# A two-level Strassen projection: another order of its products, two of its results combined in turn, and two reciprocals moved behind the score evictions

## The chip, the cores and the metric

The kernel runs on one core of a Trainium2 chip. The metric is the device time of one execution in microseconds. Below, PE is TensorE's matmul pipe and PEld its weight load, DVE is VectorE, ACT is ScalarE, POOL is GpSimd and SP is SyncE.

## The reference, cut to what matters

`x` has 64 graphs of 256 nodes with 512 features, `adj` is one 256 x 256 matrix shared by all. Everything is float32. Two layers with a residual each:

```python
h = relu(layernorm(x))
x = x + einsum('nm,bmd->bnd', adj, h) @ W0 + b0          # layer 0

h = relu(layernorm(x))                                    # layer 1, 8 heads of 64
q, k, v = h @ Wq + bq, h @ Wk + bk, h @ Wv + bv
scores = einsum('bqhd,bkhd->bhqk', q, k) / 8 + (1 - adj) * -1e9
x = x + einsum('bhqk,bkhd->bqhd', softmax(scores), v) @ Wo + bo
```

## The kernel before, in words

**Groups and halves.** The 64 graphs are worked on two at a time, in 32 groups (`NG`). Layer 0 runs over all groups first, and leaves its residual and its normalized, turned result in DRAM. Layer 1 then runs over the groups; it takes a little over 2000 us of the span, about 66.5 us for each group. This text is about layer 1.

**The projections.** Each 512 x 512 weight times the group's 512 x 512 activations is done with Winograd's form of Strassen's algorithm: seven products of half-size blocks in place of eight. `weight_sums` makes the weight sums s1 to s4, `Halves.sums` the activation differences t1 to t4. `project` (L447) does one level: P1 = a11 b11 goes to bank pa, and is read from there (u1) before more is added to it; a12 b21 makes result (0,0) with u1; s2 t2 is added to pa (u2 is read); s1 t1 goes to bank pc (c22 is read); s3 t3 is added to pa once more (u3 is read, and with c22 it makes result (1,1)); a22 t4 makes (1,0) with u3; s4 b22, added to pc, makes (0,1) with u2. In the kernel's listing P5 is the product s1 t1. A result's first index is the half of the output features, the second the graph of the pair. Because s2 t2 is added in the bank that u1 was read from, TensorE can start that product only when the reader of P1 is through.

For Q, K and V the reader is ScalarE (L756 with the bias, L777 a copy), which writes u into one of three buffers of the pool `tmp`. For the output projection (`post`, L791) the reader is VectorE, which adds the product to the residual in place (L600).

**The second level.** From group 4 on (`FIRST2`), the three products of Q, K and V that are used once (a12 b21, a22 t4, s4 b22) are themselves done by seven quarter-size products, in `project2` (L559), `product2` (L527, matmuls at L538) and `finish2` (L540). `product2` writes what several quarters share to a bank `shared`, the rest to the bank `own`. `finish2` then makes the result by five adds on VectorE (`add`, L599), each of which reads what the one before wrote: own plus u over 512 elements, a shared part onto 512, onto 384, onto 256, and the last onto 128 (or 256 for s4 b22, whose bank pc already held s1 t1).

**Attention.** A group has two halves of four heads, `qd` 0 and 1. `attend` (L849) sums the exponents over the keys on TensorE (pden, L856), multiplies them with V (pav, L863, into two banks `po`), reads the sums with ScalarE (L870) and makes reciprocals of them on VectorE, in four calls of 128 columns (L873). A closure `divide` is queued for the next tick: it multiplies `po` with the reciprocals (L880), gives its two banks back, has ScalarE add up the reciprocals for a check of range (L882), and starts the differences that the output projection needs. `score` (L814) makes the scores in banks (L824), moves each 128 x 512 bank to SBUF with scale and mask on VectorE (L829, eight evictions), subtracts a bound on GpSimd (L835), takes the exponent on ScalarE (L840) and adds pairs of keys on GpSimd (L847).

**Order.** All instructions are put in order by hand: each engine runs its own in the order in which the program makes them. Generators yield between products; `run` calls `tick` at each yield, and `after(n, f)` has f emitted n ticks later. For group g the main loop (L946) does: `attend(g, 0)`, `score(g, 1)`, a tick (so `divide` comes right behind the score), Q and K of group g+1, `attend(g, 1)`, `score(g+1, 0)`, a tick, V of group g+1, and the output projection `post(g)`. Around the end of that loop, group 31 has no next Q, K, V; `post(30)` runs in their place.

**Banks.** PSUM's eight banks are handed out first in, first out by `bank` and `give` while the program is made; an instruction that writes a bank waits on the chip for the last reader of its earlier tile.

The functions that the change touches, with what calls them:

Of the kernel before, what the change touches and what calls it, by code (L numbers as in the profile page):

```python
# [198 lines left out]
def kernel(  # L199
# [24 lines left out]
    NG = B // GB  # L224
# [21 lines left out]
    def bank(shape, name):  # L246
        i = free_banks.pop(0)
        t = psum.tile(shape, F32, tag=f"bank{i}", name=name)
        bank_of[id(t)] = (i, t)
        return t  # L250

    def give(t):
        free_banks.append(bank_of.pop(id(t))[0])
# [35 lines left out]
    def quarter(xt, i, k):  # L289

        return xt[:, k * NT:(k + 1) * NT, i * HF:(i + 1) * HF]
# [111 lines left out]
    W = {}  # L403
# [35 lines left out]
    def product(ps, s, a, halves, b, by_token, start=True, stop=True):  # L439
        for m in range(2):  # L440
            for c in range(2):
                w, y = s[a][:, c, :], halves.operand(b, c)
                lhs, rhs = (y[:, m * P:(m + 1) * P], w) if by_token else (w[:, m * P:(m + 1) * P], y)
                nc.tensor.matmul(ps[:, m, :], lhs, rhs, start=(start and m + c == 0), stop=(c == 1),  # L444
                                 skip_group_check=True)

    def project(s, halves, by_token, name, read, finish, first_half_first=False):  # L447


        def new(n):  # L450
            return bank([P, 2, N], f"{name}{n}")
        pa = new("a")
        product(pa, s, "a11", halves, "b11", by_token, stop=False)
        u1 = read(pa, 1)
        yield
        if first_half_first:
            pc = new("c")
            product(pc, s, "s1", halves, "t1", by_token, stop=False)
            c22 = read(pc, 0)
            yield  # L460
        pb = new("b")
        product(pb, s, "a12", halves, "b21", by_token)
        finish(pb, u1, 0, 0)
        give(pb)
        yield
        product(pa, s, "s2", halves, "t2", by_token, start=False, stop=False)
        u2 = read(pa, 2)
        yield
        if not first_half_first:
            pc = new("c")  # L470
            product(pc, s, "s1", halves, "t1", by_token, stop=False)
            c22 = read(pc, 0)
            yield
        product(pa, s, "s3", halves, "t3", by_token, start=False)
        u3 = read(pa, 3)
        finish(pa, c22, 1, 1)
        give(pa)
        yield
        pd = new("d")
        product(pd, s, "a22", halves, "t4", by_token)  # L480
        finish(pd, u3, 1, 0)
        give(pd)
        yield
        product(pc, s, "s4", halves, "b22", by_token, start=False)
        finish(pc, u2, 0, 1)
        give(pc)
        yield
# [6 lines left out]
    FIRST2 = 4  # L494
# [45 lines left out]
    def finish2(o, own, shared, u, by_token, fresh):  # L540

        def quarters(t):
            return t.rearrange("p m (n k) -> p (m n) k", k=P)

        def spread(i, n):
            return shared[:, i:i + 1, :].to_broadcast([P, n, P])
        add(o, own, u)
        q = quarters(o)
        lower = q[:, 1::2, :] if by_token else q[:, 2:4, :]
        right = q[:, 2:4, :] if by_token else q[:, 1::2, :]  # L550
        add(q, spread(0, 4), q)
        add(q[:, 1:4, :], spread(1, 3), q[:, 1:4, :])
        add(lower, spread(2, 2), lower)
        if fresh:
            add(right[:, 0, :], quarters(own)[:, 3, :], right[:, 0, :])
        else:
            add(right, spread(3, 2), right)

    def project2(n, halves, blocks, by_token, name, read, target):  # L559

        s = W[n]

        def new(i):
            return bank([P, 2, N], f"{name}{i}")

        def once(own, a, i, k, u, fresh):
            shared = bank([P, 4, P], f"{name}r")
            product2(own, shared, W2[n, a], blocks[ONCE[a]], by_token, fresh)
            finish2(target(i, k), own, shared, u, by_token, fresh)
            give(own)  # L570
            give(shared)

        pa = new("a")
        product(pa, s, "a11", halves, "b11", by_token, stop=False)
        u1 = read(pa, 1)
        yield
        pc = new("c")
        product(pc, s, "s1", halves, "t1", by_token, stop=False)
        c22 = read(pc, 0)
        yield  # L580
        product(pa, s, "s2", halves, "t2", by_token, start=False, stop=False)
        u2 = read(pa, 2)
        yield
        once(new("b"), "a12", 0, 0, u1, True)
        yield
        product(pa, s, "s3", halves, "t3", by_token, start=False)
        u3 = read(pa, 3)
        add(target(1, 1), pa, c22)
        give(pa)
        yield  # L590
        once(new("d"), "a22", 1, 0, u3, True)
        yield
        once(pc, "s4", 0, 1, u2, False)
        yield

    def partial(name, n):
# [2 lines left out]
    def add(o, ps, u):  # L599
        nc.vector.tensor_tensor(o, ps, u, op=ALU.add)  # L600
# [187 lines left out]
    def quarter_of(batch, i):  # L788
        return batch.rearrange("(t p) d -> p t d", p=P)[:, :, i * HF:(i + 1) * HF]

    def post(g):  # L791

        xt = X.pop(g)
        halves = HO.pop(g)
        done = []

        def read(ps, n):
            o = quarter(xt, *RESIDUAL[n])
            add(o, ps, o)

        def finish(ps, u, i, k):
            o = quarter(xt, i, k)
            add(o, ps, o)
            done.append(k)
            if g == NG - 1:
                nc.sync.dma_start(quarter_of(out[g * GB + k], i), o)
            elif done.count(k) == 2:
                nc.sync.dma_start(out[g * GB + k].rearrange("(t p) d -> p t d", p=P), xt[:, k * NT:(k + 1) * NT, :])

        yield from project(W["o"], halves, True, f"o_{g}", read, finish, first_half_first=g == NG - 1)  # L810

    A, AS = {}, {}

# [35 lines left out]
    def attend(g, qd):  # L849


        pd = bank([P, GN], f"pden_{g}_{qd}")
        po = [bank([P, GN], f"pav_{g}_{qd}_{f}") for f in range(2)]
        for b in range(GB):
            for h in range(4):
                nc.tensor.matmul(pd[h * 32:(h + 1) * 32, b * N:(b + 1) * N], ones[:, 0:32], AS[h // 2, b][:, h % 2, :],  # L856
                                 start=True, stop=True, tile_position=(0, h * 32))
        for b in range(GB):
            v = V[g][qd, b]
            for k in range(NT):  # L860
                for f in range(2):
                    for h in range(4):
                        nc.tensor.matmul(po[f][h * 32:(h + 1) * 32, b * N:(b + 1) * N],  # L863
                                         v[:, k, h * HD + f * 32:h * HD + f * 32 + 32],
                                         A[h // 2, b][:, (h % 2) * NT + k, :],
                                         start=(k == 0), stop=(k == NT - 1), tile_position=(0, h * 32))
        i = g * HQ + qd
        dens = act.tile([P, 2, GN], F32, tag="yT1", name=f"den_{g}_{qd}")
        den, rden = dens[:, 0, :], dens[:, 1, :]
        nc.scalar.activation(den, pd, AF.Identity, accum_out=stats[:, 0, i:i + 1])  # L870
        give(pd)
        for c in range(4):
            nc.vector.reciprocal(rden[:, c * P:(c + 1) * P], den[:, c * P:(c + 1) * P])  # L873
        if qd == 0:
            OT[g] = act.tile([P, DC, GN], F32, tag="r", name=f"oT_{g}")
            HO[g] = Halves(f"o_{g}", [OT[g][:, :, k * N:(k + 1) * N] for k in range(GB)], 1)

        def divide():
            for f in range(2):
                nc.vector.tensor_tensor(OT[g][:, 2 * qd + f, :], po[f], rden, op=ALU.mult)  # L880
                give(po[f])
            nc.scalar.activation(den, rden, AF.Identity, accum_out=stats[:, 1, i:i + 1])  # L882
            if g < NG - 2 or qd == 0:
                HO[g].sums(nc.gpsimd if g < NG - 1 else nc.vector, ("t1",) if qd == 0 else ("t2", "t3", "t4"))
            elif g == NG - 2:
                after(9, HO[g].sums, nc.gpsimd, ("t2", "t3", "t4"))
            else:
                HO[g].sums(nc.vector, ("t2",))
                after(1, HO[g].sums, nc.vector, ("t3", "t4"))

        after(1 if g < NG - 1 or qd else 8, divide)

    def run(gen, steps=99):
# [129 lines left out]
```

## Time and profile before

| what | value |
|---|---|
| time, median of 3 runs | 2771.95 us (2771.8 to 2772.26) |
| span of the profiled execution | 2769.3 us |
| L829 evictions, 512 of them | 310.2 us, 678 ns each |
| L873 reciprocals, 256 of 128 x 128 | 216.5 us, 908 ns each |
| L882 sums of the reciprocals, 64 | 40.3 us, 630 ns each |
| L870 sums over the keys, 64 | 38.2 us, 597 ns each |

A row of the timeline has the start, the length, the engine, the line, the operation, what it writes and reads, their shapes, and a count; rows of one kind that follow each other are merged, and lengths overlap a little where an engine starts the next instruction before the last has ended. What stands in brackets is idle time of the engine just before the row, and what ended it. Matmuls of float32 show as two rows each, so that 8 rows are a product's four matmuls of 256 columns. Lines named L600 are VectorE's add, whoever calls it: the names of the tiles tell the caller (q, k, v: `finish2`; x: the output projection).

### The profile page before, as it was taken

To read this page: it belongs to the slowest core of one execution; us is meant where nothing else is said; L and a number is where in the kernel's file an instruction comes from. 1 tells how busy PE (TensorE), PEld (TensorE's weight loads), DVE (VectorE), ACT (ScalarE), POOL (GpSimd) and SP (SyncE) were. 2 spreads that over 40 slices of the span, in tenths; PEclk is the share of its full clock that TensorE was granted. 3 is DMA by queue.
4 is the path that set the end of the run, shared out by engine and by line. 5 is a ranking of instruction groups with operands and counts; after the bars stand their busy time and mean duration, and the time that the engine had idled before them with its cause. 6 is when DMAs were issued, how large, how long until landed. Compare 5 with 4: busy or idle time off the path is not lost.

```text
span 2769.3 us, 47852 instructions
## 1 busy us (share of the span) xinstructions
PE 2690.7 (97%) x18684; PEld 2271.7 (82%) x18684; DVE 2002.4 (72%) x3789; ACT 875.6 (32%) x1537; POOL 1961.6 (71%) x1630
## 2 busy tenths in 40 slices
PE   8999999999999999999999999999999999999998
PEld 7888888887888888888888888888888888888886
DVE  7777777865446777777777777777777777777776
ACT  3434344343332222333222222222333222222221
POOL 6777776675777667777777777667777777666665
PEclk9999999999999999999999999999999999999999
DMA  7776666662111111111111112222211111111110
GB/s 187 191 192 166 160 169 161 172 151 68 46 47 46 47 47 47 47 47 47 47 47 46 47 47 54 57 60 56 51 47 47 47 47 47 47 47 47 47 47 32
DMA packets 281045, 210.78 MB, mean 76 GB/s; under 512 B 145904, under 2 KB 212976, under 8 KB 280816
## 3 DMA queue, kind: packets, MB, share of 16 engines
q1 hardware_dynamic: 280352, 207.15, 29.0%
q8 instruction: 150, 2.46, 0.4%
q10 hardware_dynamic: 464, 0.52, 0.1%
q14 instruction: 79, 0.65, 0.1%
HBM read 106.96 MB, written 100.66 MB: 75 GB/s over the span
## 4 chain that ended last, share of the span: by engine, by line
PE 67%; POOL 17%; DVE 14%; issue 1%; DMA 0%; POOLq 0%; ACT 0%; DVEq 0%; SPq 0%; ACTq 0%
POOL a L835 10%; DVE k L600 9%; PE py L646 8%; PE sc L824 5%; PE pav L863 4%; POOL as L847 4%; DVE den L873 4%; POOL t_o L437 3%; PE pden L856 1%; DVE a L829 1%; DVE x L600 1%; DVE v L600 0%; PE q_27a L444 0%; PE q_25a L444 0%; PE q_19a L444 0%
## 5 line engine op out<-in xcount | busy, mean ns | idle before, releaser
L835 POOL TENSOR_TENSOR a<-a,top 128x1024 f32<-128x1024 f32 x254 | 594.3, 2370 | 593.2 <-DVE a L829 593.2
L829 DVE SCALAR_TENSOR_TENSOR a<-sc,maskT 128x512 f32<-128x512 f32 x512 | 310.2, 678 | 15.4 <-PE sc L824 15.4
L847 POOL TENSOR_TENSOR as<-a 128x512 f32<-128x512 f32 x256 | 318.0, 1276 | 0.7 <-DVE r L682 0.7
L824 PE MATMUL sc<-q,k 64*128 64x256 f32 x2048 | 262.8, 387 | 17.4 <-DVE a L829 17.4
L840 ACT ACTIVATE a<-a 128x1024 f32<-128x1024 f32 x256 | 264.6, 1057 | 23.9 <-POOL a L835 23.9
L824 PEld LDWEIGHTS sc<-q,k 64*128 64x128 f32 x2048 | 199.2, 186 | 81.5 <-DVE a L829 37.1
L873 DVE RECIPROCAL den<-den 128x128 f32<-128x128 f32 x256 | 216.5, 908 | 36.2 <-ACT den L870 36.1
L863 PE MATMUL pav<-a,v 128*32 128x256 f32 x4096 | 233.3, 379 | 0.5 <-DVE v L600 0.5
L646 PE MATMUL py<-adjT,h 128*128 128x256 f32 x1024 | 229.0, 382 | 0.9 <-DVE adjT L325 0.9
L870 ACT ACTIVATE den<-pden 128x512 f32<-128x512 f32 x64 | 38.2, 597 | 604.0 <-PE pden L856 592.8
L646 PEld LDWEIGHTS py<-adjT,h 128*128 128x128 f32 x1024 | 196.2, 192 | 28.7 <-ACT h L621 1.2
L863 PEld LDWEIGHTS pav<-a,v 128*32 128x32 f32 x4096 | 133.4, 110 | 88.8 <-issue 1.0
L676 ACT ACTIVATE h<-x,nb,rs 128x512 f32<-128x512 f32 x128 | 97.1, 806 | 318.3 <-POOL nb L54 318.3
L954 POOL TENSOR_TENSOR x<-x,bo_r 128x512 f32<-128x512 f32 x128 | 159.9, 1292 | 13.0 <-DVE x L600 13.0
L53 POOL TENSOR_TENSOR rs<-rs,mhalf 128x2 f32<-128x2 f32 (+1 forms) x97 | 78.5, 810 | 123.1 <-DVE nb L52 123.1
L625 POOL TENSOR_TENSOR x<-x,b_r 128x512 f32<-128x512 f32 x128 | 159.8, 1283 | 1.0 <-ACT h L621 0.9
L882 ACT ACTIVATE den<-den 128x512 f32<-128x512 f32 x64 | 40.3, 630 | 280.0 <-DVE den L873 280.0
L437 POOL TENSOR_TENSOR t_y<-yT,t_y 128x256 f32<-128x256 f32 (+1 forms) x96 | 87.5, 911 | 41.4 <-ACT yT L656 38.9
L697 DVE BATCH_NORM_STATS2 st<-x 128x6 f32<-128x256 f32 x256 | 96.4, 418 | 4.4
L621 ACT ACTIVATE h<-x,nb,rs 128x512 f32<-128x512 f32 x128 | 93.9, 806 | 10.4 <-POOL nb L54 10.4
L42 DVE BATCH_NORM_STATS2 st<-x 128x6 f32<-128x512 f32 x128 | 85.6, 669 | 6.6 <-DMA x<-in_x_dram 6.6
L437 POOL TENSOR_TENSOR t_y<-yT 128x256 f32<-128x256 f32 (+1 forms) x96 | 88.7, 924 | 2.2 <-ACT yT L656 0.9
(5610 smaller groups left out, 6472.7 us busy)
## 6 DMA issues: line engine op xcount, KB each, us to landing
x<-in_x_dram SPq DMA_DIRECT2D x256, 128.0 KB, 3.5
residual<-x SPq DMA_DIRECT2D x256, 128.0 KB, 2.3
hidden<-r SPq DMA_DIRECT2D x128, 256.0 KB, 4.6
h1T<-hidden SPq DMA_DIRECT2D x64, 512.0 KB, 9.3
x<-residual SPq DMA_DIRECT2D x32, 1024.0 KB, 6.4
out_dram<-x SPq DMA_DIRECT2D x62, 512.0 KB, 3.2
w_sb<-in_L_gnn_weight_dram SPq DMA_DIRECT2D x1, 1024.0 KB, 9.8
wq_sb<-in_L_gnn_Wq_dram SPq DMA_DIRECT2D x1, 1024.0 KB, 7.9
```

The costliest lines, as they stand in the source:

```text
L437: eng.tensor_tensor(self.t[n][:, c, :], self.operand(p, c), self.operand(q, c), op=ALU.subtract)
L600: nc.vector.tensor_tensor(o, ps, u, op=ALU.add)
L625: nc.gpsimd.tensor_tensor(xt[:, t, :], xt[:, t, :], b0_r, op=ALU.add)
L646: nc.tensor.matmul(pss[d][:, b * N:(b + 1) * N], h[:, b * NT + k, d * P:(d + 1) * P], adjT[:, k, :], start=(k == 0), stop=(k == NT - 1))
L824: nc.tensor.matmul(ps[j][:, kt * N:(kt + 1) * N], k[j * HD:(j + 1) * HD, c, kt * P:(kt + 1) * P], q[j * HD:(j + 1) * HD, c, :], start=True ...
L829: nc.vector.scalar_tensor_tensor(a[:, j * NT:(j + 1) * NT, :].rearrange("p k n -> p (k n)"), ps[j], SCALE, maskT_f, op0=ALU.mult, op1=ALU.add)
L835: nc.gpsimd.tensor_tensor(a, a, top_b, op=ALU.subtract)
L840: nc.scalar.activation(a, a, AF.Exp)
L847: nc.gpsimd.tensor_tensor(AS[c, b], a4[:, :, 0, :], a4[:, :, 1, :], op=ALU.add)
L863: nc.tensor.matmul(po[f][h * 32:(h + 1) * 32, b * N:(b + 1) * N], v[:, k, h * HD + f * 32:h * HD + f * 32 + 32], A[h // 2, b][:, (h % 2) * ...
L873: nc.vector.reciprocal(rden[:, c * P:(c + 1) * P], den[:, c * P:(c + 1) * P])
L954: after(9 + t, lambda t, xt: nc.gpsimd.tensor_tensor(xt[:, t, :], xt[:, t, :], L1["o"][1], op=ALU.add), t, X[g])
```

## The change

Four edits, with one aim: what TensorE waits for should be ready sooner.

1. `finish2` returns its five adds as a list. A new function `finish_all` emits the lists of one or more results in turn, one add of each, and gives the banks back.
2. `project2` moves the product s4 b22 from the end to the fourth place, just ahead of a12 b21, and combines those two results in turn with `finish_all`. a22 t4 becomes the last product. Result (0,1) is so made together with (0,0), which is the order in which the scores and attention want them.
3. `post` calls `project` with `first_half_first=True` in all groups (before: in the last only). The product s1 t1 (P5) then comes right behind P1, and s2 t2, which must wait for P1's reader, one product later.
4. `attend`, from group 4 on, makes two of the four reciprocals at once and leaves two to `divide`, so that they stand behind the evictions of the score that comes between. The last call of all, (31, 1), still makes four at once.

```diff
-        add(o, own, u)
         q = quarters(o)
...
-        add(q, spread(0, 4), q)
-        add(q[:, 1:4, :], spread(1, 3), q[:, 1:4, :])
-        add(lower, spread(2, 2), lower)
-        if fresh:
-            add(right[:, 0, :], quarters(own)[:, 3, :], right[:, 0, :])
-        else:
-            add(right, spread(3, 2), right)
+        return [(o, own, u), (q, spread(0, 4), q), (q[:, 1:4, :], spread(1, 3), q[:, 1:4, :]),
+                (lower, spread(2, 2), lower),
+                (right[:, 0, :], quarters(own)[:, 3, :], right[:, 0, :]) if fresh else (right, spread(3, 2), right)]
...
+        def finish_all(*products):
+            for ops in zip(*(ops for _, _, ops in products)):
+                for op in ops:
+                    add(*op)
+            for own, shared, _ in products:
+                give(own)
+                give(shared)
...
         u2 = read(pa, 2)
         yield
-        once(new("b"), "a12", 0, 0, u1, True)
+        c12 = once(pc, "s4", 0, 1, u2, False)
+        yield
+        c11 = once(new("b"), "a12", 0, 0, u1, True)
+        finish_all(c12, c11)
         yield
         product(pa, s, "s3", halves, "t3", by_token, start=False)
         u3 = read(pa, 3)
         add(target(1, 1), pa, c22)
         give(pa)
         yield
-        once(new("d"), "a22", 1, 0, u3, True)
-        yield
-        once(pc, "s4", 0, 1, u2, False)
+        finish_all(once(new("d"), "a22", 1, 0, u3, True))
         yield
...
-        yield from project(W["o"], halves, True, f"o_{g}", read, finish, first_half_first=g == NG - 1)
+        yield from project(W["o"], halves, True, f"o_{g}", read, finish, first_half_first=True)
...
-        for c in range(4):
+
+        def invert(c):
             nc.vector.reciprocal(rden[:, c * P:(c + 1) * P], den[:, c * P:(c + 1) * P])
+
+        early = 2 if g >= FIRST2 and (g, qd) != (NG - 1, 1) else 4
+        for c in range(early):
+            invert(c)
...
         def divide():
+            for c in range(early, 4):
+                invert(c)
             for f in range(2):
                 nc.vector.tensor_tensor(OT[g][:, 2 * qd + f, :], po[f], rden, op=ALU.mult)
                 give(po[f])
```

More of the change, by code (lines that the diff above doesn't have):

```diff
@@ L568, in once @@
             product2(own, shared, W2[n, a], blocks[ONCE[a]], by_token, fresh)
-            finish2(target(i, k), own, shared, u, by_token, fresh)
-            give(own)
-            give(shared)
+            return own, shared, finish2(target(i, k), own, shared, u, by_token, fresh)
+        def finish_all(*products):
[5 more added lines that the diff above has]
+                give(shared)
         pa = new("a")
```

## The prediction, made before the changed kernel had run

> **What bounds the kernel now.** I read the page's engine shares first, then TensorE's timeline over one group of the second layer, then the timelines of the two engines that it waits for, and last the busy time of one period.
>
> ```profile
> span 2769.3 us, 47852 instructions
> PE 2690.7 (97%) x18684; PEld 2271.7 (82%) x18684; DVE 2002.4 (72%) x3789; ACT 875.6 (32%) x1537; POOL 1961.6 (71%) x1630
> 1497.03:1563.50 66.47, 64.59 (x507) 54.10 (x503) 49.16 (x85) 19.43 (x36) 47.58 (x34) 1.00 0.19 49
> ```
>
> TensorE is busy 97% of the span. The third line (length, then PE, PEld, DVE, ACT, POOL busy, granted clock, DMA share, GB/s) is one group's period, 66.47 us, at full clock. So a change helps only by closing a gap on PE, and hurts as soon as it opens one.
>
> ```profile
> 1517.65 1.89 PE L444 MATMUL o_12b<-wo_sb,oT 128*128 128x256 f32 x8
> 1520.80 1.97 PE L444 MATMUL o_12a<-wo_s,t_o 128*128 128x256 f32 x8 [1.26 <-DVE x L600]
> ...
> 1534.06 3.73 PE L824 MATMUL sc<-q,k 64*128 64x256 f32 x32
> 1537.71 1.99 PE L444 MATMUL q_14a<-h1T,wq_sb 128*128 128x256 f32 x8
> 1539.54 1.89 PE L444 MATMUL q_14c<-t_h,wq_s 128*128 128x256 f32 x8
> 1541.27 1.89 PE L444 MATMUL q_14a<-t_h,wq_s 128*128 128x256 f32 x8
> ...
> 1565.55 2.86 PE L824 MATMUL sc<-q,k 64*128 64x256 f32 x24
> 1569.03 1.72 PE L824 MATMUL sc<-q,k 64*128 64x256 f32 x8 [0.62 <-DVE a L829]
> 1570.69 1.99 PE L444 MATMUL v_14a<-wv_sb,h1T 128*128 128x256 f32 x8
> ```
>
> There are two gaps per group. Gap A: the scores after K take 1570.69 - 1565.55 = 5.14 us, the others 1537.71 - 1534.06 = 3.65, so 1.49 is lost; the row shows only 0.62 of it, since a matmul's end is modelled and the last banks come one eviction at a time. Gap B: the output projection's third product could start at 1517.65 + 1.73 = 1519.38 (products follow each other at 1.73) and starts at 1520.80: 1.42 lost. The wait table counts A 28 times and B once for each of o_3 to o_29, 27 times.
>
> ```profile
> 1531.46 3.39 DVE L873 RECIPROCAL den<-den 128x128 f32<-128x128 f32 x4 [1.06 <-ACT den L870]
> 1535.29 4.88 DVE L829 SCALAR_TENSOR_TENSOR a<-sc,maskT 128x512 f32<-128x512 f32 x8 [0.44 <-PE sc L824]
> 1540.08 1.28 DVE L880 TENSOR_TENSOR oT<-pav,den 128x512 f32<-128x512 f32 x2
> ...
> 1562.94 2.20 DVE L600 TENSOR_TENSOR k<-k_14r,k 128x512 f32<-128x512 f32 x4
> 1565.06 3.38 DVE L873 RECIPROCAL den<-den 128x128 f32<-128x128 f32 x4
> 1568.35 4.81 DVE L829 SCALAR_TENSOR_TENSOR a<-sc,maskT 128x512 f32<-128x512 f32 x8
> ```
>
> ```profile
> 1534.94 0.63 ACT L882 ACTIVATE den<-den 128x512 f32<-128x512 f32 x1 [3.51 <-DVE den L873]
> 1535.48 0.19 ACT L882 ACTIVATION_READ_ACCUMULATOR den<-den 128x1 f32 x1
> 1539.74 0.84 ACT L756 ACTIVATE u_q<-q_14a,bq_c 128x256 f32<-128x256 f32 x2 [4.08 <-PE q_14a L444]
> ```
>
> After K, VectorE still works off K's results until 1565.06, then four reciprocals, and only then the evictions that free banks for the scores. Before Q, the reciprocals end 0.44 us before the first score bank is there: nothing is to be gained. The last view matters most: ScalarE's sum of the reciprocals (L882) starts 0.09 us after the fourth reciprocal, and stands in its queue directly ahead of the read of Q's (or V's) first product, u1.
>
> [...] L882 idles 3.51 us and nothing passes it. [...] a dependent pair of 512-element adds starts 0.72 apart (1562.22, 1562.94), eight independent evictions 0.60 apart (4.88 for 8)[...]. [...] with two banks held for attention's output the scores stop after 24 of 32 rows, six banks.
>
> **The change part by part.**
>
> *Alternating, s4 product moved up.* A group's three projections do the same 48 adds on VectorE and the same matmuls. Alternated, the two five-op chains are independent: about 0.12 us saved for each of some 8 pairs, near 1 us. Against it, the second result's first op waits in VectorE's queue for its product, 1.56 us after the first's: about 0.9 idle. For K, counted from its start at 1549.41: first op 1556.4, second 1558.0, nine spaced steps (0.60, 0.60, 0.60, 0.47, 0.47, 0.33, 0.33, 0.33, 0.20: 0.60 for 512 elements and 0.19 for 128 are in the trace, between them in proportion) to 1561.9, the fourth quarter's add 0.60, then the last chain's 2.6: 1565.1, as before. Cost and gain: nothing, the backlog after a projection stays 15.7 us from its start. The compiled order's banks free in time, with attention's second output bank closest: about 0.2 us to spare.
>
> *P5 second in the output projection.* One product of 1.73 us comes between P1 and the third product. The add that frees P1's bank comes at the same time after V as before, so gap B (1.42) closes with 0.3 to spare: 27 x 1.42 = 38.3 gained. o_30 waits 4.6 us for GpSimd instead and gains 1.7.
>
> *Two reciprocals behind the scores, g = 4 to 30.* At K's end two reciprocals less take 1.65 us off: evictions could start at 1565.06 + 1.66 = 1566.7, about when the first score bank is complete (in the other scores 1535.29 - 1534.06 = 1.23 after their start: 1566.8). The seventh bank is needed at 1568.3 and is free at 1567.5. Gap A closes: 27 x 1.49 = 40.2 gained.
>
> The cost is on ScalarE. Its sum of the reciprocals reads all four, so it now stands behind eight evictions and two reciprocals, and ahead of u1. The third product of Q and V adds into the bank that u1 reads, and TensorE's queue waits there, everything behind it too. The compiled order of the changed kernel has exactly this: sum, then u1, and the third product waiting on ScalarE.
>
> Q: evictions end 1540.17, reciprocals three and four from 1540.08 take 1.75 (row of two: 0.82 + 0.91), to 1541.83; sum from 1541.92, with its accumulator read 0.73, to 1542.65; u1 0.84 to 1543.49; 0.14 until PE goes on (seen at gap B: add ends 1520.66, PE 1520.80): 1543.63. Due 1541.27. New wait 2.36.
>
> V: evictions 1566.78 to 1571.66, two reciprocals to 1573.3, sum to 1574.1, u1 as one copy of 0.59 to 1574.75, PE at 1574.9. Due 1570.69 - 1.49 + 3.55 = 1572.75. New wait 2.1.
>
> Sum per group: -1.49 - 1.42 + 2.36 + 2.1 = +1.55, so the period goes from 66.47 to about 68.0. 27 x 1.55 = 41.9, less 1.7 for o_30: +40. Predicted 2771.95 + 40 = 2812. The multiplication by the reciprocals ends at 1543.1 and disturbs nobody: VectorE idles until 1544.8 now, and Q's first op comes later still.
>
> **The rivals.**
>
> 1. *ScalarE does not hold TensorE up* (the order on chip lets u1 go first). Then both gaps close for nothing: 27 x 2.91 + 1.7 = 80, 2692 us, faster. For it: ScalarE is only 32% busy. Against: the in-order wait at L882 is visible, and the product's wait on u1 is in the program. Chance 0.06.
> 2. *The waits balance.* If each new wait were 1.45, all would cancel: 2770. It needs evictions or reciprocals 0.8 us quicker than their rows; both are steady in the trace. Chance 0.03.
> 3. *A gap stays as well.* If waits inside the alternated chain cost 0.04 each, it ends 0.4 later, V's wait grows by as much and gap B keeps up to 0.2; if B stayed whole, 1.4. That gives +0.5 to +1.4 per group, 2826 to 2850. For it: 0.3 to spare is little. Chance 0.15.
> 4. *As worked out*, 0.76, with 0.3 us per group either way for latencies I read to a tenth: 2804 to 2820.
>
> **How the numbers follow.** 2812 is case 4. The range, 2800 to 2830, holds case 4 and the near half of case 3, over 8 in 10. Slower by over 0.2%: 0.76 + 0.15 = 0.91; same 0.03; faster 0.06.
>
> **What would show it.** In TensorE's waits of the changed kernel, the 27 of the o products on the residual add and most of the 28 of the scores on their evictions should be gone, and the third products of q and v for groups 5 to 31 should wait for ScalarE's u, 2.4 and 2.1 us (less in the row, since ends are modelled). The sum on ScalarE should start near the end of the evictions. Evictions after K should start about 1.6 us sooner against their scores. A period near 66.5 or below, or no ScalarE waits on TensorE, would make me wrong; o products that still wait would point to case 3.

## The result, and the profile after

The changed kernel takes 2857.28 us (2854.74 to 2857.55, 4 runs) against 2771.91 us: ratio 1.0306, 95% interval 1.0288 to 1.0324. It is slower, as forecast, but by 85 us where 40 were forecast. The page's head, its chain and one of its groups of instructions:

```profile
span 2853.0 us, 47741 instructions
PE 2695.8 (94%) x18684; PEld 2274.0 (80%) x18684; DVE 1958.9 (69%) x3789; ACT 864.7 (30%) x1537; POOL 1958.1 (69%) x1630
...
PE 72%; DVE 22%; ACT 3%; POOL 2%; issue 1%; DMA 0%; ACTq 0%; DVEq 0%; POOLq 0%
...
L891 ACT ACTIVATE den<-den 128x512 f32<-128x512 f32 x64 | 40.3, 630 | 611.0 <-DVE den L876 611.0
```

The last two lines, the chain and ScalarE's sum of the reciprocals, as they were before:

```profile
PE 67%; POOL 17%; DVE 14%; issue 1%; DMA 0%; POOLq 0%; ACT 0%; DVEq 0%; SPq 0%; ACTq 0%
L882 ACT ACTIVATE den<-den 128x512 f32<-128x512 f32 x64 | 40.3, 630 | 280.0 <-DVE den L873 280.0
```

TensorE does the same work (2695.8 us busy, 2690.7 before), in a span 84 us longer. ScalarE has 3% of the chain where it had none, and its sum of the reciprocals (L891, L882 before) idles 611 us ahead of itself where it idled 280. TensorE's timeline over one group:

```profile
1567.78 1.99 PE L444 MATMUL q_14a<-h1T,wq_sb 128*128 128x256 f32 x8
1569.61 1.89 PE L444 MATMUL q_14c<-t_h,wq_s 128*128 128x256 f32 x8
1573.60 1.97 PE L444 MATMUL q_14a<-t_h,wq_s 128*128 128x256 f32 x8 [2.09 <-ACT u_q L758]
...
1597.96 3.73 PE L826 MATMUL sc<-q,k 64*128 64x256 f32 x32
1601.61 1.99 PE L444 MATMUL v_14a<-wv_sb,h1T 128*128 128x256 f32 x8
1603.44 1.89 PE L444 MATMUL v_14c<-wv_s,t_h 128*128 128x256 f32 x8
1607.08 1.99 PE L444 MATMUL v_14a<-wv_s,t_h 128*128 128x256 f32 x8 [1.75 <-ACT u_v L779]
...
1618.78 1.89 PE L444 MATMUL o_13b<-wo_sb,oT 128*128 128x256 f32 x8
1620.51 1.89 PE L444 MATMUL o_13a<-wo_s,t_o 128*128 128x256 f32 x8
1623.27 1.97 PE L444 MATMUL o_13a<-wo_sb,t_o 128*128 128x256 f32 x8 [0.88 <-DVE x L602]
```

Both old gaps are closed: the scores after K take 1601.61 - 1597.96 = 3.65 us, and the output projection's third product follows the second at 1.73. Three new gaps are there. Products follow each other at 1.73, so q's third was due at 1571.34 and is 2.26 late, v's at 1605.17 and is 1.91 late, and the output projection's fifth at 1622.24, 1.03 late. The next rows, from ScalarE's and VectorE's timelines, show why q's is late:

```profile
1572.00 0.63 ACT L891 ACTIVATE den<-den 128x512 f32<-128x512 f32 x1 [10.50 <-DVE den L876]
1572.54 0.19 ACT L891 ACTIVATION_READ_ACCUMULATOR den<-den 128x1 f32 x1
1572.63 0.82 ACT L758 ACTIVATE u_q<-q_14a,bq_c 128x256 f32<-128x256 f32 x2
```

```profile
1565.36 4.88 DVE L831 SCALAR_TENSOR_TENSOR a<-sc,maskT 128x512 f32<-128x512 f32 x8 [2.06 <-PE sc L826]
1570.15 1.75 DVE L876 RECIPROCAL den<-den 128x128 f32<-128x128 f32 x2
```

The sum waits 10.50 us for the two reciprocals behind the evictions, and u1 waits behind the sum. And there is a loss that no wait shows. Below are three stretches of 3.40 us; q's wait in group 15, which ends at 1642.55, lies in the first (columns: length, busy time of PE, PEld, DVE, ACT and POOL, granted clock, DMA share, GB/s):

```profile
1639.90:1643.30 3.40, 1.30 (x7) 0.85 (x6) 2.25 (x4) 2.35 (x7) 3.40 (x3) 1.00 0.03 4
1643.40:1646.80 3.40, 3.40 (x14) 2.96 (x13) 0.00 (x0) 1.95 (x4) 3.40 (x3) 0.50 0.02 5
1646.80:1650.20 3.40, 3.40 (x27) 3.29 (x27) 1.55 (x3) 2.40 (x3) 3.40 (x4) 1.00 0.02 5
```

```profile
1642.55 2.94 PE L444 MATMUL q_15a<-t_h,wq_s 128*128 128x256 f32 x8 [2.10 <-ACT u_q L758]
```

For 3.4 us the clock is halved from 0.8 us after the wait on, and the product behind it takes 2.94 us where that of group 14 above took 1.97. That happens behind 10 of the 27 waits of q, and such a group takes 70.61 us (third product of q_7 to that of q_8, 1085.97 to 1156.58) in place of 68.95.

The sum: the period went from 66.47 to 68.95. From the start of q_5 to that of q_31 there are 26 periods, and 26 x 2.48 is 64.5; the half clock of ten groups, at 1.66 each, is 16.6; together 81.1. That stretch took 1728.1 us before and takes 1809.2 now, 81.1 more, out of the 83.7 by which the two spans differ. Of the rest, 3.9 come between q_0 and q_5, and ahead of q_0, where the programs do not differ, it is 1.1 less. Edit 3 acts between q_0 and q_5 too, on the output projections of groups 0 to 2: TensorE had no wait there before, now it has the new one, and from q_2 to q_3 it takes 66.07 us where it took 64.96:

```profile
796.70 1.97 PE L444 MATMUL o_1a<-wo_sb,t_o 128*128 128x256 f32 x8 [0.88 <-DVE x L602]
```

### The profile page after: what moved, and what is told of

It is laid out like the page before. It is cut to its first block, busy times and chain, and to the rows that moved or that the text cites. A ratio compares the mean times of both kernels' runs of the same rounds, so it can differ in the third digit from the quotient of the medians.

```text
span 2853.0 us, 47741 instructions
## 1 busy us (share of the span) xinstructions
PE 2695.8 (94%) x18684; PEld 2274.0 (80%) x18684; DVE 1958.9 (69%) x3789; ACT 864.7 (30%) x1537; POOL 1958.1 (69%) x1630
## 4 chain that ended last, share of the span: by engine, by line
PE 72%; DVE 22%; ACT 3%; POOL 2%; issue 1%; DMA 0%; ACTq 0%; DVEq 0%; POOLq 0%
DVE a L831 9%; PE py L648 8%; DVE k L602 7%; DVE den L876 5%; PE pav L865 4%; PE sc L826 2%; ACT den L891 1%; PE pden L858 1%; POOL a L837 1%; DVE x L602 1%; ACT u_q L758 1%; ACT u_v L779 0%; DVE v L602 0%; PE o_18a L444 0%; PE o_6a L444 0%
## 5 line engine op out<-in xcount | busy, mean ns | idle before, releaser
L876 DVE RECIPROCAL den<-den 128x128 f32<-128x128 f32 x256 | 223.7, 919 | 36.2 <-ACT den L872 36.0
L826 PE MATMUL sc<-q,k 64*128 64x256 f32 x2048 | 239.2, 383 | 0.6 <-DVE a L831 0.6
L891 ACT ACTIVATE den<-den 128x512 f32<-128x512 f32 x64 | 40.3, 630 | 611.0 <-DVE den L876 611.0
```

The lines of the kernel that those rows point to most:

```text
L826: nc.tensor.matmul(ps[j][:, kt * N:(kt + 1) * N], k[j * HD:(j + 1) * HD, c, kt * P:(kt + 1) * P], q[j * HD:(j + 1) * HD, c, :], start=True ...
```

## The experiments

Each was timed against the kernel before on the same chip. "The theory" in the expectations is the account above; rival 1 blames VectorE's lateness, rival 2 the alternated adds.

**Only the sum's place.** ScalarE's sum is emitted three ticks later, everything else as in the changed kernel:

```diff
-            nc.scalar.activation(den, rden, AF.Identity, accum_out=stats[:, 1, i:i + 1])
+            def total():
+                nc.scalar.activation(den, rden, AF.Identity, accum_out=stats[:, 1, i:i + 1])
+            if FIRST2 <= g < NG - 1:
+                after(3, total)
+            else:
+                total()
```

> The changed kernel with one thing moved: for groups 4 to 30 ScalarE's sum of the reciprocals is emitted three ticks later, behind the reads of the first three products. Theory (the sum's place in ScalarE's queue holds u1, and with it the third product): the waits of q and v on ScalarE go, the half-clock stretches behind q's wait go with them, the period falls from 68.95 by 2.26 and 1.91 to 64.8 us, the time to 2725 us. Rival 1 (VectorE is late, because two reciprocals stand behind the evictions): nothing changes, about 2857 us. Rival 2 (the alternated adds cost the excess): the waits go, but some 45 us stay, about 2770 us.

Measured 2723.71 us, ratio 0.9825 (0.9809 to 0.9841). The place of this one instruction was worth 134 us. The waits of q and v are gone, and with them the half clock behind them (mean clock 0.998). ScalarE's timeline of this kernel shows the sum behind u2, where nobody waits for it, and TensorE's has one wait left in a group:

```profile
1562.41 0.58 ACT L779 COPY u_v<-v_14a 128x512 f32<-128x512 f32 x1 [0.24 <-PE v_14a L444]
1562.89 1.06 ACT L842 ACTIVATE a<-a 128x1024 f32<-128x1024 f32 x1
1563.85 0.62 ACT L892 ACTIVATE den<-den 128x512 f32<-128x512 f32 x1
```

```profile
1573.75 1.89 PE L444 MATMUL o_13a<-wo_s,t_o 128*128 128x256 f32 x8
1576.52 1.97 PE L444 MATMUL o_13a<-wo_sb,t_o 128*128 128x256 f32 x8 [0.88 <-POOL t_h L437]
```

Both rivals fall. The wait that is left is that of the output projection's fifth product. The row names GpSimd, with a tile that this product does not read (it reads t_o). GpSimd's last t_o and VectorE's add of the third product, from their timelines:

```profile
1567.64 1.29 POOL L437 TENSOR_TENSOR t_o<-oT,t_o 128x512 f32<-128x512 f32 x1
1575.67 0.69 DVE L602 TENSOR_TENSOR x<-o_13a,x 128x512 f32<-128x512 f32 x1 [1.03 <-PE o_13a L444]
```

The t_o is there at 1568.93, more than 7 us early. The add ends at 1576.36, and the fifth product starts 0.16 later: it is the add that frees pa.

**All four reciprocals early** (`early = 4` in the changed kernel: edits 1 to 3 alone).

> The changed kernel with all four reciprocals ahead of the evictions again. Theory: no wait of q and v on ScalarE, no half-clock stretches, the scores after K lose their 1.49 us per group again, the output projection still loses 1.04 between its third and fifth product in place of 1.42: 27 times 0.38 and 1.7 for o_30 less than before, 2760 us. Rival 1: the same. Rival 2 (the alternated adds cost some 45 us): about 2805 us.

Measured 2761.69 us, ratio 0.9965 (0.9951 to 0.9979). As the theory has it: without the moved reciprocals the rest of the change is a small gain.

**Each edit alone on the kernel before.** First the reciprocals' (edit 4):

> The kernel before with the reciprocals' edit alone. Theory: per group -1.49 at the scores after K, +2.26 at q, +1.91 at v, 27 times 2.68 is 72, and 0 to 20 us of half clock: 2844 to 2864 us. Rival 2: the excess belongs to the alternated adds, so 40 us more than before at most, 2812 us.

Measured 2876.45 us, ratio 1.0376 (1.0359 to 1.0394). The waits are those of the theory, 2.1 for q and 1.7 to 1.8 for v in the rows, but there is more half clock than I allowed: the mean clock is 0.988, and 16 of the 27 waits of q are followed by it: 16 x 1.66 is 27 us where at most 20 were allowed. Another 5 are in the period without half clock, 69.33 where the theory gives 69.15. Then the output projection's (edit 3, `first_half_first=True`):

> The kernel before with the output projection's edit alone. Theory: the wait of the third product (1.42) is traded for one between the third and the fifth, which now follow each other on one bank (1.04): 27 times 0.38 and 1.7 less, 2760 us. Rival (the recorded prediction's step: the gap just closes): 27 times 1.42 and 1.7 less, 2732 us.

Measured 2761.83 us, ratio 0.9964 (0.9950 to 0.9978). The prediction's step, that the gap just closes, falls; it is traded for a shorter one. The rows in TensorE's timeline:

```profile
1586.60 1.89 PE L444 MATMUL o_13b<-wo_sb,oT 128*128 128x256 f32 x8
1588.33 1.89 PE L444 MATMUL o_13a<-wo_s,t_o 128*128 128x256 f32 x8
1591.10 1.97 PE L444 MATMUL o_13a<-wo_sb,t_o 128*128 128x256 f32 x8 [0.88 <-POOL t_h L437]
```

Third (1588.33) right behind the second, fifth (1591.10) 2.77 behind the third: 1.04 late. And the second level's order and alternated adds (edits 1 and 2):

> The kernel before with the order of products and the alternated adds alone. Theory: VectorE is through with a projection as late as before, so no gap of TensorE changes: 2770 us, within 5. Rival 2 (the alternated adds cost the excess): 2800 us and more.

Measured 2770.55 us, ratio 0.9997 (0.9988 to 1.0005): no difference, as expected.

**Shorter waits.** Three reciprocals early, one late:

```diff
-        early = 2 if g >= FIRST2 and (g, qd) != (NG - 1, 1) else 4
+        early = 3 if g >= FIRST2 and (g, qd) != (NG - 1, 1) else 4
```

> The changed kernel with three reciprocals ahead of the evictions and one behind. Theory: q's wait falls by one reciprocal from 2.26 to 1.44 us; v's stays at 1.91, since there the evictions start later by what is taken away behind them; the scores after K stay closed to some 0.2: 27 times 1.7 more than before, 2816 us, and no half-clock stretch, since no wait is as long as 2.26. Rival (half clock comes from the number of waits, not from their length): some ten stretches as now, 2833 us.

Measured 2813.21 us, ratio 1.0150 (1.0133 to 1.0167). The time fits, and no wait of q or v is followed by half clock (mean clock 0.998, as in the kernel before), with as many waits as in the changed kernel, so the rival falls. One term was wrong: v's wait fell too, to 0.96 in the row, and the scores ahead of it kept more of theirs:

```profile
1583.71 4.34 PE L826 MATMUL sc<-q,k 64*128 64x256 f32 x32
...
1592.66 1.99 PE L444 MATMUL v_14a<-wv_s,t_h 128*128 128x256 f32 x8 [0.96 <-ACT u_v L779]
```

4.34 for the scores against 3.73: what the third reciprocal takes there, v's product comes later and so waits less. After K, as long as one reciprocal stays behind the evictions, VectorE has the same work ahead of the sum: the sum starts 8.24 us after the first reciprocal here (1583.17 to 1591.41) and 8.42 in the changed kernel (1597.41 to 1605.83).

**One wait at a time.** The sum is moved only where Q follows (condition `qd == 0` added), so that v's wait stays:

> The changed kernel with the sum moved only where Q follows; v keeps its wait of 1.91 us. Theory: -1.49 - 0.38 + 1.91 is nothing, and a wait of 1.9 brings no half clock: 2771 us, the clock as before. Rival (v's waits bring half clock as q's do): ten stretches of 1.66 us more, 2788 us.

Measured 2777.85 us, ratio 1.0023 (1.0016 to 1.0031), mean clock 0.998. No wait of v is followed by half clock, so the rival falls; the expectation was 6 us short. Against the kernel before, the profiled run has 3.9 us more between q_0 and q_5, as the changed kernel has, and 3.9 more up to q_31, from a period of 66.62 in place of 66.47; elsewhere it has 2 less. The other way round, q's wait stays:

> The changed kernel with the sum moved only where V follows; q keeps its wait of 2.26 us. Theory: 27 times (-1.49 - 0.38 + 2.26) less 1.7 is +9, and q's waits bring half clock in about ten of the 27 groups, 1.66 us each: 2798 us, the mean clock near 0.993. Rival (half clock needs both waits close together): 2781 us, the clock as before.

Measured 2820.92 us, ratio 1.0176 (1.0159 to 1.0193), mean clock 0.985. q's wait alone brings half clock, so the rival falls here too, and not in ten groups but in 21 of 27. The 11 more, at 1.66 us, are 18 of the 23 us above the expectation.

**The fifth product moved away from the third.** Both add to bank pa. On top of the later sum, s4 b22 (bank pc) goes between them in the output projection:

```diff
+        if apart:
+            product(pc, s, "s4", halves, "b22", by_token, start=False)
+            finish(pc, u2, 0, 1)
+            give(pc)
+            yield
         product(pa, s, "s3", halves, "t3", by_token, start=False)
...
-        product(pc, s, "s4", halves, "b22", by_token, start=False)
-        finish(pc, u2, 0, 1)
-        give(pc)
-        yield
+        if not apart:
+            product(pc, s, "s4", halves, "b22", by_token, start=False)
+            finish(pc, u2, 0, 1)
+            give(pc)
+            yield
...
-        yield from project(W["o"], halves, True, f"o_{g}", read, finish, first_half_first=True)
+        yield from project(W["o"], halves, True, f"o_{g}", read, finish, first_half_first=True, apart=g < NG - 1)
```

> The changed kernel with the sum three ticks later and, in the output projection of groups 0 to 30, the last product (s4 b22) put between the third and the fifth, which add to one bank. Theory: all four gaps close, period 68.95 - 2.26 - 1.91 - 1.04 is 63.74 us, the time 27 times 2.73 and 1.7 below before: 2697 us. Rival (VectorE's adds come too late for the product put between as well): 0.5 to 1 us per group stays, 2710 to 2725 us.

Measured 2687.77 us (2686.06 to 2688.34), ratio 0.9694 (0.9681 to 0.9708): 3.1% faster than the kernel before and 5.9% than the changed one. It is 9 us below the expectation too. The period, 63.5 us in place of 63.74, accounts for 6 of them: a product behind a wait also takes a little longer (rows of 1.97 or 1.99 above where others last 1.89), and that went with the three waits. All of the period is busy on TensorE, at full clock:

```profile
1500.00:1563.50 63.50, 63.50 (x503) 54.01 (x503) 47.67 (x85) 19.25 (x36) 47.64 (x35) 1.00 0.20 51
```

```profile
1557.69 1.89 PE L444 MATMUL o_13a<-wo_s,t_o 128*128 128x256 f32 x8
1559.41 1.89 PE L444 MATMUL o_13c<-wo_s,oT 128*128 128x256 f32 x8
1561.14 1.89 PE L444 MATMUL o_13a<-wo_sb,t_o 128*128 128x256 f32 x8
```

The products follow each other at 1.73, and the wait is gone. The rival falls.

**The same with the old order of the second level** (edits 1 and 2 undone in it):

> As the one before, with the second level's products and adds in the order of the kernel before. Theory: that order is worth nothing by itself here, so 2697 us as well, within 5. Rival (with the other gaps closed, the earlier result (0,1) or VectorE's saved microsecond counts): 5 us and more slower, in a wait of the scores on k or of the output projection on VectorE.

Measured 2691.59 us (2689.1 to 2691.92), ratio 0.9707 (0.9693 to 0.9721). That is 5.4 below the expectation and 3.8 above the run before, short of the rival's 5. The period is the same, 63.5. Of the 3.6 us between the two profiled spans, 1.9 are there before layer 1 has begun, where the programs do not differ, and 1.0 comes once, at group 31, where attention waits 0.5 us for V's result in this kernel and not in the other. So the order of edits 1 and 2 is worth 1 to 2 us here, if anything.

## Why the prediction was right in its direction and wrong in its size

Its steps, with the segments of one group before (from 1537.71) and after (from 1567.78):

| step | forecast | measured |
|---|---|---|
| q's third product waits for the sum | +2.36 | +2.26 |
| v's third product waits for the sum | +2.1 | +1.91 |
| scores after K | -1.49 | -1.49 |
| output projection | -1.42 | -0.39 |
| rest (first matmuls behind a wait) | 0 | +0.17 |
| period | +1.55 | +2.48 |
| half clock behind q's wait, all groups | 0 | +16.6 |
| output projections of groups 0 to 2, all three | 0 | +3.3 |

*The mechanism that decides the direction* was right, and the later sum shows it: ScalarE's queue holds TensorE, though ScalarE is busy 30% of the time. The two waits are within 0.2 us of what was worked out from rows of the kernel before.

*The scores after K* close as worked out, and VectorE's backlog after a projection is unchanged by the alternated adds: K's last add ends at 1597.49, 15.68 after K's start at 1581.81, where 15.7 was forecast. From q_5 to q_31 TensorE's wait table has the waits of q, v and the output projection alone; the new order of banks costs nothing there.

*"... so gap B (1.42) closes with 0.3 to spare"* is the first step that failed. I followed the wait of the third product, and it did go. But the product moved ahead, s1 t1, had stood between the third and the fifth, and both add to bank pa; now the fifth must wait for the read of the third. The time from the third's end to the end of its add and on to TensorE is 1.04 us, 27 times 28 us. Only 0.39 of the 1.42 was gained. And the edit is made in all groups, which the forecast left out: o_0 to o_2 had no gap to close, and each pays the new wait, some 3.3 us for the three.

*The clock* was not in the sum at all, the second step that failed: with full clock all through, q's wait was put at its own length, and half clock behind it in ten groups cost 17 us more. The trace of before had a hint that I passed over, the stretch behind o_30's wait of 4.6 us for GpSimd (columns as above):

```profile
2730.20:2733.60 3.40, 3.32 (x9) 2.70 (x10) 0.00 (x0) 1.44 (x3) 3.40 (x4) 0.59 0.00 0
```

I had counted on full clock from the mean of 0.998.

*o_30* keeps 2.83 of its 4.6 us, as forecast (1.7 less), but pays 1.04 at its fifth product too. Of the rivals, the third (a gap stays) named the output projection, for another cause: a late VectorE chain. Its 0.3 of slack was real; the third product does not wait. The sign "o products that still wait would point to case 3" misleads here: they do wait, at the fifth, but VectorE is not late; it idles 1.03 us ahead of the add in question, in the row of the first experiment.

Added up: +28 from the fifth product, +17 from the clock, +5 from the rest, -8 from two waits a little shorter than forecast: 42 of the 45 us that were missing. The 3.3 of the first three output projections fill the rest; that it comes out so evenly is in part luck, since smaller differences at both ends of the span cancel.

## What to carry to other kernels

When an instruction is moved later, look for what else reads its result on an engine that works in order, as ScalarE did here, and for what stands behind that reader: here two reciprocals that nobody on TensorE wanted pulled a small sum with them, and the sum stood in front of the copy that TensorE needed. When a product is moved away from one place to break a chain on a bank, check the place it leaves, and whether every round that gets the change had the gap that it is to close. A gap of TensorE can cost more than its length (2.26 us here, and 1.66 more behind 10 of the 27), so work out the waits one by one before trading two short ones for two longer ones.

## What the runs showed of the hardware

*Half clock behind a wait of 2.26 us.* The ten half-clock stretches behind q's waits on ScalarE in the changed kernel begin at 1087.0, 1295.2, 1435.2, 1643.4 and so on, and each is 3.4 us long. The kernel with the reciprocals' edit alone has 16 of them, and the one where only q waits has 21.

The length of a wait does not decide by itself. In all three kernels q's third product is 2.25 or 2.26 us late in groups 5 to 31, and still 10, 16 and 21 of the 27 waits are followed by half clock. Nor does a longer wait always bring it: in the changed kernel o_30 waits 2.99 us (2812.53 to 2815.52) and the rows behind it keep their length of 1.99 and less, where q_1 waits 2.59 (680.64 to 683.23) and its next two products take 2.83 and 2.79. Shorter waits had none behind them: v's, 1.91 us, in none of 27 groups of the changed kernel, and in the kernel with three reciprocals early neither q's nor v's (1.3 and 1.0 in the rows, mean clock 0.998). What tells the waits that are followed from those that are not was not shown: no run varied it alone.

*One wait, three counts.* In the changed kernel the groups with half clock are 7, 10, 12, 15, 17, 20, 22, 25, 28 and 30, never two in succession. With q's wait alone they come in runs: 7 to 10, 12 to 15, 17 to 20, 22 to 26 and 28 to 31. At 1.66 us each, the same wait so cost 17 us in one kernel and 35 in another.
